# The build-time clock of VectorE's queue: new spacings and waits, and polynomial work filled up to a later limit

## The chip, the core and the metric

The kernel runs on one core of a Trainium2 chip. The metric is the device time of one execution in microseconds. Before the change it is 8143.15 us, the median of three runs between 8141.27 and 8144.12.

Five engines work beside each other, each in the order in which its instructions were written: TensorE (PE, with its weight loads as PEld), VectorE (DVE), ScalarE (ACT), GpSimd (POOL) and SyncE (SP), which issues most of the DMAs.

## What is computed

The input is x of 4 x 64 x 64 x 128 (batch, height, width, channels). Two layers follow each other; each image becomes 4096 tokens of 128 channels. Cut to what matters:

```python
# layer 0
c1 = conv3x3(elu(x), W1) + b1
a, b = split(conv3x3(c1, W2) + b2)
c3 = a * sigmoid(b)
q, k, v = c3 @ Wq + bq, c3 @ Wk + bk, c3 @ Wv + bv      # 4, 4 and 16 wide
x = x + c3 + tile(causal_softmax(q k^T / 4) @ v, 8) @ W3 + b3
# layer 1, on tokens
y = layernorm(x)
h = y + softmax(heads(y wq) heads(y wk)^T) heads(y wv) @ wo    # 16 heads of 8, not causal
t = x + h + (silu(h @ w1) * (h @ w3)) @ w2
z = layernorm(t)
p = softmax(z @ router_w + router_b)
out = t + sum over the two best experts e of p_e / (p_1 + p_2) * (z @ expert_w[e] + expert_b[e])
```

The costliest part is the exponential of the 16-head attention: 4 images x 16 heads x 4096 x 4096 scores.

## The kernel before

**The stream of attention steps.** The second attention is cut into segments. A segment is one image b, one group g of four heads and one chunk c of 512 queries. It has 32 steps, one for each tile of 128 keys; a few segments of the first image are shorter. A step multiplies four heads' keys with the queries (four matmuls into two PSUM tiles `s` of 128 x 1024), lets ScalarE take the exponential of both (`e<-s`), and, one or two steps later, multiplies values with `e` into the sum `acc`, which lies in one PSUM bank of its own. `s` has three buffers. The first attention's steps (36 for each image) go through the same stream.

**Polynomial.** In each segment of 32 steps, one key tile (number 20) is left out of ScalarE's work. Its exponential is worked out by VectorE instead: this is the class `Beside`. A job has four units, one for each head, and two halves. A unit is one matmul into the single bank `m` and one VectorE operation `ey<-m`; behind it eight steps on 128 x 512 elements are put on the list `beside_todo` (round off, fraction, to power, first, three terms, last). When all four units are ready, the two halves multiply the values with the four tiles `ey` into `acc`.

**Fillers.** All other work of the layers is written as Python generators, which yield between pieces: convolutions and first attention of the next image (`PREPARE`, 138.5 us of PE in the planner's units), and for each image and chunk a `last_part` (`LAST`, 18.3): output projection, gated feed-forward, LayerNorm, router, gates, experts. Within the stream, every piece of a filler uses the same single bank `m`. A yield names its cost and a kind: `held` (the bank is in use over the yield), `stop`, `free` (nothing on PE).

**The planner's turn.** The loop at the end of `fast_path` writes the order by hand while the program is built. A turn is one step; `turn_at` goes on by `EXPS`, 1.81 us. In a turn come, in this order: the scores of the step; one piece, either of a job (`can[0].piece()`) or of a filler (`insert()`); the values of an earlier step (`finish(2)`); the jobs' ages (`step()`); and `beside_work(until)`, which takes polynomial steps from the list as long as VectorE's clock plus the step's cost stays under `until`. A piece needs an empty bank (`empty`), some credit, and room on PE (`left >= PIECE`, or a credit over 1.5); in the first two turns of a segment none is issued (`quiet`). A half needs its polynomial to be done by the clock: `done_at <= turn_at[0] + 0.4`. Halves that are not out by the last step are forced there by `beside_rest`, and pieces that are left when the stream ends run alone.

**The clocks.** `InOrder` keeps each engine's instructions in the order written. For VectorE it calls `dve_time` at each instruction, which moves `dve_at`, the estimated end of VectorE's queue; `pool_time` does so for `pool_at`. `bank_at` is the estimated end of VectorE's last read of bank `m`. None of these puts a wait into the program; the semaphores for real dependencies are there in any case. They only settle which instruction comes where.

**Places that the text below uses.** `layernorm` (`ve`, then `rs` on GpSimd, then four operations that read `rs`); `top` and the gates in `last_part` (some 17 operations on 32 elements in front of the first `by_e`); the experts (`by_e<-m`, twice for each of four tiles, with a sum after the second); `elu` in the convolutions.

All trace lines carry L113, the line of the helper that records every instruction, so tiles name them.

Of the kernel before, what the change touches and what calls it, by code (L numbers as in the profile page):

```python
# [21 lines left out]
NQ = N // QB  # L22
# [103 lines left out]
def fast_path(ctx: ExitStack, tc: tile.TileContext, a: dict, where: dict, out: bass.AP, verdict):  # L126
# [7 lines left out]
    x = a["x"]  # L134
# [3 lines left out]
    turn_at, dve_at, pool_at, bank_at = [0.0], [0.0], [0.0], [0.0]  # L138

    def pool_time(name, args):  # L140

        aps = [x for x in args if hasattr(x, "shape")]
        if aps and name != "dma_start":
            took = 0.65 + 1.25e-3 * int(np.prod(aps[0].shape[1:]))
            pool_at[0] = max(pool_at[0], turn_at[0] + 0.5) + took

    def dve_time(name, args):

        aps = [x for x in args if hasattr(x, "shape")]
        from_bank = any(x.name.startswith("m_") or x.name == "m" for x in aps)  # L150
        from_sums = any(x.name.startswith("acc") for x in aps)
        in_sbuf = not any(x.space == bass.MemoryType.PSUM for x in aps)
        took = max(int(np.prod(x.shape[1:])) for x in aps[:2]) / 960.0
        if in_sbuf and name in ("tensor_scalar", "tensor_copy"):
            took *= 0.5
        if name == "tensor_reduce" and aps[1].ap[-1][0] != 1:
            took *= 1.8
        begins = turn_at[0] + (0.95 if from_bank else 1.75 if from_sums else 0.0)
        if in_sbuf and max(dve_at[0], begins) < pool_at[0]:
            took += 0.75  # L160
        dve_at[0] = max(dve_at[0], begins) + 0.07 + took
        if from_bank:
            bank_at[0] = dve_at[0]

    dve, pool = InOrder(tc, nc.vector, dve_time), InOrder(tc, nc.gpsimd, pool_time)

    const = ctx.enter_context(tc.tile_pool(name="f_const", bufs=1))
# [12 lines left out]
    def m_tile():  # L180
        return ps_m.tile([P, QB], FP, tag="m", name="m")
# [7 lines left out]
    def chunk(tag, name=None):  # L189
        return wk.tile([P, QB], FP, tag=tag, bufs=CHUNKS.get(tag, 1), name=name or tag)  # L190

    def small(name, dims):
        return sm.tile([P, *dims], FP, tag=name, name=name)

    def by_k(ap):
        return ap.rearrange("p (k c) -> p k c", k=4)
# [63 lines left out]
    acc = ps_o.tile([P, QB], FP, tag="acc", name="acc")  # L260
# [7 lines left out]
    bank_held = [False]  # L268

    def do_step(step):  # L270
        scores, values = step
        undone.append((values, scores()))

    def finish(leave):
        while len(undone) > leave:
            values, es = undone.pop(0)
            values(es)
# [10 lines left out]
    def insert():  # L288

        while fillers:  # L290
            r = advance(fillers[0])
            if r is not None:
                return r[0]
            fillers.pop(0)
        return 0.0

    def layernorm(t, y):

        t, y = by_k(t), by_k(y)
        mv = sm.tile([P, 4, 2], FP, tag="mv", name="mv")  # L300
        for k in range(4):
            st = sm.tile([P, 6], FP, tag="st", name="st")
            dve.bn_stats(st, t[:, k, :])
            dve.bn_aggr(mv[:, k, :], st)
        ve = small("ve", [4])
        dve.tensor_scalar(ve, mv[:, :, 1], LN_EPS, None, ALU.add)
        rs = small("rs", [4])
        pool.tensor_tensor(rs, ve, minus_half, ALU.pow)
        dve_at[0] += 1.2
        for k in range(4):  # L310
            dve.tensor_scalar(y[:, k, :], t[:, k, :], mv[:, k, 0:1], rs[:, k : k + 1], ALU.subtract, ALU.mult)

# [624 lines left out]
    beside_todo = []  # L937

    class Beside:
# [27 lines left out]
        def unit(self, j):  # L967
            ps = m_tile()
            r = slice(j * SLOT, (j + 1) * SLOT)
            pe.matmul(  # L970
                ps,
                lhsT=kx[r, self.place * P : (self.place + 1) * P].bitcast(FR),
                rhs=self.qx[r, :].bitcast(FR),
                start=True,
                stop=True,
            )
            y = chunk("ey")
            self.e.append(y)
            dve.tensor_scalar(y, ps, LOG2E, None, ALU.mult)
            low, a = [], [-((-1) ** k) * POWER[k] / float(np.float32(POWER[5])) for k in range(5)]  # L980

            def round_off():
                low.extend([chunk("em"), chunk("part", "eg")])
                dve.tensor_scalar(low[0], y, TO_WHOLE + EXPONENT, None, ALU.add)

            def fraction():
                dve.scalar_tensor_tensor(low[1], low[0], TO_WHOLE + EXPONENT, y, ALU.subtract, ALU.subtract)

            def to_power():
                whole = low[0].bitcast(mybir.dt.int32)  # L990
                dve.tensor_scalar(whole, whole, 23, MANTISSA, ALU.logical_shift_left, ALU.bitwise_or)

            def first():
                dve.scalar_tensor_tensor(y, low[1], a[4], low[1], ALU.add, ALU.mult)

            def term(k):
                return lambda: dve.scalar_tensor_tensor(y, y, a[k], low[1], ALU.add, ALU.mult)

            def last():
                dve.scalar_tensor_tensor(y, y, a[0], low[0], ALU.add, ALU.mult)  # L1000
                self.ready += 1
                self.done_at = dve_at[0]

            beside_todo.extend([(0.35, round_off), (0.6, fraction), (0.35, to_power), (0.6, first)])
            beside_todo.extend([(0.6, term(3)), (0.6, term(2)), (0.6, term(1)), (0.6, last)])

        def half(self, h):
            kt = self.kt
# [9 lines left out]
    def beside_work(until, beside_pool=True):  # L1018
        while beside_todo and dve_at[0] + beside_todo[0][0] <= until:
            if not beside_pool and max(dve_at[0], turn_at[0] + 0.5) < pool_at[0]:  # L1020
                break
            beside_todo.pop(0)[1]()
# [206 lines left out]
    batches = []  # L1229
# [121 lines left out]
    jobs = []  # L1351
# [107 lines left out]
    while True:  # L1459
        turn_at[0] += EXPS  # L1460
        if steps_in:
            do_step(steps_in.pop(0))
        else:
            step = next(steps, False)
            if step is False:
                break
            waiting = step is None
            if waiting:
                finish(0)
            else:  # L1470
                do_step(step)
        b = now[0]
        if batches[b].second == NQ and len(batches) == b + 1 and b + 1 < B:
            Batch(b + 1)
            begun = 0
            while begun < len(fillers) and (fillers[begun][2] in fetching or fillers[begun][2] is None):
                begun += 1
            fillers.insert(begun, [first_attention(b + 1, batches[b + 1]), PREPARE, None, False])

        rate = 1.0  # L1480
        if batches[b].second == NQ:
            later = PREPARE * (B - len(batches)) + LAST * (last_parts_left[0] - 1)
            rate = (sum(part[1] for part in fillers) + later) / max(1, sum(steps_left) - 40)
        credit = min(3.0, credit + rate)
        left = ahead + EXPS - SCORES - (VALUES if len(undone) > 2 else 0.0)
        free = bool(fillers) and fillers[0][3]
        turn = not quiet[0] and free and not waiting
        if turn:
            took = insert()
            credit -= took  # L1490
            left -= took
        can = [job for job in jobs if job.can() and (left >= PIECE or job.late())]
        empty = bank_held[0] or bank_at[0] <= turn_at[0] + 0.5 or batches[b].second < NQ
        if can and empty and not (quiet[0] or bank_held[0] or steps_in or waiting):
            can[0].piece()
            left -= PIECE
        elif not turn and (waiting or not quiet[0] and empty and credit > 0.0 and (left >= PIECE or credit > 1.5)):
            took = insert()
            credit -= took
            left -= took  # L1500
        ahead = min(max(left, 0.0), AHEAD)
        finish(2)
        for job in jobs:
            job.step()
        beside_work(turn_at[0] + 2.5, any(job.age > 3 * job.units + 4 for job in jobs if job.halves < 2))
    finish(0)
    alone[0] = True
    run_alone([(r for part in fillers for r in part[0])], lambda: False)
# [678 lines left out]
def conv_attn_hybrid_kernel(tc: tile.TileContext, a: dict, where: dict, out: bass.AP):  # L2187
    nc = tc.nc
    with tc.tile_pool(name="verdict", bufs=1) as pool:
        verdict = pool.tile([1, 1], FP, name="verdict")  # L2190
        fast_path(tc, a, where, out, verdict)

        beyond = nc.values_load(verdict.bitcast(mybir.dt.int32))
        with tc.If(beyond > 0x3F800000):
            general_path(tc, a, where, out)
# [30 lines left out]
```

## Time and profile before

| what | us |
|---|---|
| median of three runs | 8143.15 |
| the profiled execution | 8143.47 |
| its span, first to last instruction | 8141.6 |
| PE busy (73,465 matmuls) | 7864.7 |
| ACT busy (8,459 instructions) | 7690.0 |
| of it the exps `e<-s`, 8,256 | 7626.4 |
| DVE busy (9,289 instructions) | 4802.6 |
| POOL busy | 671.3 |
| granted TensorE clock | 0.988 |

The table gives busy time over the whole span. The stream of attention steps begins near 200 us and ends at 8049 us; ahead of it lie weights, the first bands of the convolution and the first chunks, behind it what is left of the fillers. PE's busy time overstates it, since matmuls are pipelined and their ends are modelled.

In the views, a wait line reads: engine and tile that waited, what released it, microseconds in total, how many times, the longest. A timeline line has start, duration, engine, operation, output and input, and in brackets the idle time before it with what ended it. `PEld` is a weight load, the first thing of a product that can wait.

### The profile page before, as it was taken

Reading aid. Unit: us, or ns where it says so; the run is one execution under the profiler, and the core shown is the slowest. Engines: PE = TensorE matmul, PEld = TensorE weight load, DVE = VectorE, ACT = ScalarE, POOL = GpSimd, SP = SyncE. Lnnn points to the kernel's source line nnn. Section 1 sums busy time; section 2 is a strip of 40 time slices with the busy share of each in tenths; the row PEclk is TensorE's granted clock in tenths of the full one; section 3 lists DMA queues with packets and bytes.
Section 4 is the critical chain, followed back from the end, with each engine's and each line's share of the span. In section 5 each row is a group of like instructions: output and inputs, shape, how many; then the busy total and the mean of one; then the engine's idle time right before and its main releaser. Section 6 shows DMA issues by size and latency. Waiting matters only on the chain. (4 is left out here: it accounts for less than half of the span.)

```text
span 8141.6 us, 177397 instructions
## 1 busy us (share of the span) xinstructions
PE 7864.7 (97%) x73465; PEld 2456.6 (30%) x73465; DVE 4802.6 (59%) x9289; ACT 7690.0 (94%) x8459; POOL 671.3 (8%) x592
## 2 busy tenths in 40 slices
PE   7999999999999999999999999999999999999997
PEld 3232222222232223223323222223233333333333
DVE  4333555463567666556656676655656666665666
ACT  1899999999999999999999999999999999999995
POOL 1211210100012110000002210000000000000000
PEclk9999999999999999999999999999999999999998
DMA  2221010101100101011010011101101111111221
GB/s 72 68 67 65 26 58 29 60 29 62 38 29 12 51 29 47 27 48 33 27 36 25 27 37 39 48 27 49 29 22 55 52 47 47 56 51 44 71 79 33
DMA packets 332340, 356.55 MB, mean 44 GB/s; under 512 B 146083, under 2 KB 222339, under 8 KB 331523
## 3 DMA queue, kind: packets, MB, share of 16 engines
q1 hardware_dynamic: 327507, 343.35, 13.3%
q8 instruction: 578, 9.47, 0.5%
q10 hardware_dynamic: 4016, 1.77, 0.1%
q14 instruction: 239, 1.96, 0.1%
HBM read 209.24 MB, written 135.79 MB: 42 GB/s over the span
## 5 line engine op out<-in xcount | busy, mean ns | idle before, releaser
L113 ACT ACTIVATE e<-s 128x1024 f32<-128x1024 f32 x8256 | 7626.4, 1085 | 222.7 <-PE s L113 214.9
L113 PE MATMUL acc<-e,vg 128*9 128x512 f32 x31872 | 4242.6, 597 | 3.4 <-DVE at L113 3.4
L113 PE MATMUL s<-qx,f_kx 32*128 32x512 f32 (+1 forms) x16512 | 2667.5, 496 | 38.5 <-DMA f_kx<-d_k 19.3
L113 PEld LDWEIGHTS s<-qx,f_kx 32*128 32x128 f32 (+1 forms) x16512 | 1080.2, 182 | 3883.5 <-ACT e L113 3612.8
L113 DVE SCALAR_TENSOR_TENSOR ey<-ey,eg 128x512 f32<-128x512 f32 x1344 | 953.9, 710 | 36.7
L113 PEld LDWEIGHTS acc<-e,vg 128*9 128x9 f32 x31872 | 727.8, 90 | 801.3 <-issue 407.2
L113 DVE COPY at<-acc 128x512 f32<-128x512 f32 x131 | 90.6, 691 | 662.4 <-PE acc L113 650.7
L113 PE MATMUL m<-v,f_wino 128*32 128x256 f32 x5376 | 429.8, 391 | 16.9 <-POOL v L113 7.3
L113 PE MATMUL m<-f_we,y2T 128*32 128x256 f32 x3840 | 308.9, 394 | 42.4 <-DVE by_e L113 28.2
L113 DVE TENSOR_SCALAR ey<-m 128x512 f32<-128x512 f32 x448 | 306.1, 683 | 68.9 <-PE m L113 65.5
L113 POOL TENSOR_TENSOR rs<-ve,f_minus_half 128x4 f32<-128x4 f32 x64 | 65.2, 1019 | 3168.5 <-DVE ve L113 3168.5
L113 DVE SCALAR_TENSOR_TENSOR ey<-ey,em 128x512 f32<-128x512 f32 x448 | 316.9, 707 | 10.2
L113 DVE SCALAR_TENSOR_TENSOR eg<-em,ey 128x512 f32<-128x512 f32 x448 | 313.2, 699 | 12.3
L113 DVE SCALAR_TENSOR_TENSOR ey<-eg 128x512 f32<-128x512 f32 x448 | 314.6, 702 | 0.0
L113 POOL TENSOR_TENSOR v<-r 128x1024 f32<-128x1024 f32 x112 | 220.6, 1975 | 1110.6 <-PE m L113 1110.1
L113 DVE COPY sd<-m 128x512 f32<-128x512 f32 x168 | 115.9, 690 | 278.3 <-PE m L113 277.4
L113 DVE TENSOR_TENSOR by_e<-m,gates 128x512 f32<-128x512 f32 x240 | 164.7, 686 | 163.8 <-PE m L113 160.1
L113 PE MATMUL m<-hT,f_fw 128*32 128x256 f32 (+1 forms) x2640 | 228.4, 391 | 0.1
L113 PE MATMUL m<-qx,f_kx 32*128 32x512 f32 x448 | 194.6, 434 | 25.1 <-DVE ey L113 23.7
L113 POOL TENSOR_TENSOR t<-t,h 128x512 f32<-128x512 f32 x32 | 43.5, 1360 | 2112.2 <-DVE h L113 2112.2
L113 DVE TENSOR_SCALAR em<-ey 128x512 f32<-128x512 f32 x448 | 196.6, 439 | 12.4
L113 DVE TENSOR_SCALAR em<-em 128x512 int32<-128x512 int32 x448 | 195.9, 437 | 10.2
(260 smaller groups left out, 4265.6 us busy)
## 6 DMA issues: line engine op xcount, KB each, us to landing
f_kx<-d_k SPq DMA_DIRECT2D x139, 512.0 KB
qx<-d_q SPq DMA_DIRECT2D x152, 256.0 KB
d_q<-two SPq DMA_DIRECT2D x64, 512.0 KB
d_a<-at SPq DMA_DIRECT2D x128, 256.0 KB
vg<-d_v SPq DMA_DIRECT2D x32, 576.0 KB
d_k<-two SPq DMA_DIRECT2D x32, 512.0 KB
d_v<-vc SPq DMA_DIRECT2D x32, 288.0 KB
xe<-in_x_dram SPq DMA_DIRECT2D x32, 256.0 KB
```

The lines of the kernel that those rows point to most:

```text
L113: made = op(*args, **kw)
```

## The change

`dve_time` gets other numbers and other cases:

- each operation costs 0.075 us beside its elements (0.07 before), and 0.117 more if it reads what the operation just before it on VectorE wrote;
- the factor of 1.8 for strided reductions is gone;
- an operation that reads bank `m` begins at 1.1 us of the turn (0.95 before), one that reads `acc` at 1.85 (1.75). New: one that reads `e` at 2.2, and LayerNorm's operations that read `rs` at 1.3 us after the estimated end of `ve` (before, `layernorm` added a flat 1.2 us to the clock);
- only inputs, no longer the output, decide of these cases;
- the supplement of 0.75 us beside GpSimd is given if the operation begins 0.2 us or more before GpSimd's end.

Six of the eight polynomial steps of each unit have a cost of 0.73 instead of 0.6 for the test in `beside_work`. The bank counts as empty if it is read by 0.3 us into the turn (0.5 before), and polynomial is filled up to 2.9 us instead of 2.5. The instructions themselves, their number and their operands stay as they are.

```diff
+    power_at, before = [0.0], [None]
+
     def dve_time(name, args):
 
         aps = [x for x in args if hasattr(x, "shape")]
-        from_bank = any(x.name.startswith("m_") or x.name == "m" for x in aps)
-        from_sums = any(x.name.startswith("acc") for x in aps)
+
+        def reads(prefix):
+            return any(x.name.startswith(prefix) for x in aps[1:])
+
+        from_bank = reads("m_") or any(x.name == "m" for x in aps[1:])
         in_sbuf = not any(x.space == bass.MemoryType.PSUM for x in aps)
         took = max(int(np.prod(x.shape[1:])) for x in aps[:2]) / 960.0
         if in_sbuf and name in ("tensor_scalar", "tensor_copy"):
             took *= 0.5
-        if name == "tensor_reduce" and aps[1].ap[-1][0] != 1:
-            took *= 1.8
-        begins = turn_at[0] + (0.95 if from_bank else 1.75 if from_sums else 0.0)
-        if in_sbuf and max(dve_at[0], begins) < pool_at[0]:
+        took += 0.075
+        if any(x.name == before[0] for x in aps[1:]):
+            took += 0.117
+        before[0] = aps[0].name
+        begins = 0.0
+        if from_bank:
+            begins = turn_at[0] + 1.1
+        elif reads("acc"):
+            begins = turn_at[0] + 1.85
+        elif reads("e_"):
+            begins = turn_at[0] + 2.2
+        elif reads("rs_") and name == "tensor_scalar":
+            begins = power_at[0] + 1.3
+        begins = max(dve_at[0], begins)
+        if in_sbuf and begins < pool_at[0] - 0.2:
             took += 0.75
-        dve_at[0] = max(dve_at[0], begins) + 0.07 + took
+        dve_at[0] = begins + took
+        if aps[0].name.startswith("ve_"):
+            power_at[0] = dve_at[0]
         if from_bank:
             bank_at[0] = dve_at[0]
...
         pool.tensor_tensor(rs, ve, minus_half, ALU.pow)
-        dve_at[0] += 1.2
...
-            beside_todo.extend([(0.35, round_off), (0.6, fraction), (0.35, to_power), (0.6, first)])
-            beside_todo.extend([(0.6, term(3)), (0.6, term(2)), (0.6, term(1)), (0.6, last)])
+            beside_todo.extend([(0.35, round_off), (0.73, fraction), (0.35, to_power), (0.73, first)])
+            beside_todo.extend([(0.73, term(3)), (0.73, term(2)), (0.73, term(1)), (0.73, last)])
...
-        empty = bank_held[0] or bank_at[0] <= turn_at[0] + 0.5 or batches[b].second < NQ
+        empty = bank_held[0] or bank_at[0] <= turn_at[0] + 0.3 or batches[b].second < NQ
...
-        beside_work(turn_at[0] + 2.5, any(job.age > 3 * job.units + 4 for job in jobs if job.halves < 2))
+        beside_work(turn_at[0] + 2.9, any(job.age > 3 * job.units + 4 for job in jobs if job.halves < 2))
```

## The prediction

> **What bounds the kernel now.** I read the page's busy table first, then busy time by stretch of the span, then the waits, then single stalls in the timeline. The table alone says little (PE 97%, ACT 94%). By stretch it is clear:
>
> ```profile
> core 0: us, PE busy (x) PEld busy (x) DVE busy (x) ACT busy (x) POOL busy (x), PEclk, DMA share, GB/s
> 2000.00:3000.00 1000.00, 968.66 (x8992) 292.69 (x8992) 660.42 (x1192) 967.24 (x1062) 135.16 (x103) 0.99 0.10 31
> 6000.00:7000.00 1000.00, 984.79 (x9920) 309.55 (x9916) 625.18 (x1242) 986.30 (x1088) 21.09 (x25) 1.00 0.16 48
> 8050.00:8141.60 91.60, 51.81 (x210) 39.07 (x208) 56.78 (x151) 4.24 (x8) 3.56 (x5) 0.73 0.08 24
> ```
>
> ACT is 97 to 99% busy while the stream of attention steps runs, 4% in the last 91.6 us. The number of exps is fixed, and the change alters none of it. So the time can move in two places: ACT's holes in the stream, and the tail after it. The waits from 400 to 8050 us name the holes:
>
> ```profile
> PEld s L113 <- ACT e L113: 3525.4, 4867, 1.7
> ACT e L113 <- PE s L113: 162.6, 126, 9.3
> ...
> PE m L113 <- DVE ey L113: 51.0, 69, 4.6
> PE acc L113 <- DVE ey L113: 38.7, 22, 4.6
> PE m L113 <- DVE by_e L113: 28.2, 23, 2.3
> ```
>
> The first line is health: PE waits for ACT at most steps. The second is the whole room inside the stream. The last three are its cause: PE, in order, stands behind a product that needs the one bank m (still unread by VectorE) or a finished polynomial tile ey. By stage the same view gives ACT 94.6 us from 1500 to 5500 and 41.0 from 5500 to 8050, which leaves 162.6 - 94.6 - 41.0 = 27.0 before 1500; 9.6 of that is a DMA (f_kx). One such stall, at the expert gates:
>
> ```profile
> 4180.73 0.19 DVE L113 TENSOR_TENSOR aw<-aw,pr 128x32 f32<-128x32 f32 x1
> 4180.84 0.15 DVE L113 TENSOR_TENSOR am<-am,bm 128x4 f32<-128x4 f32 x1
> 4181.03 0.18 DVE L113 RECIPROCAL am<-am 128x4 f32<-128x4 f32 x1
> 4181.24 0.19 DVE L113 TENSOR_TENSOR gates<-aw,am 128x32 f32<-128x32 f32 x1
> 4181.54 0.31 DVE L113 STREAM_TRANSPOSE turned<-gates 128x128 f32<-128x128 f32 x1
> 4181.77 0.65 DVE L113 TENSOR_TENSOR by_e<-m,gates 128x512 f32<-128x512 f32 x1
> ...
> 4182.48 0.16 PEld L113 LDWEIGHTS m<-f_we,y2T 128*32 128x32 f32 x8 [2.58 <-DVE by_e L113]
> ...
> 4185.46 1.94 ACT L113 ACTIVATE e<-s 128x1024 f32<-128x1024 f32 x2 [3.11 <-PE s L113]
> ```
>
> PE was sent to the bank while VectorE still worked through 17 small operations in front of by_e (4178.05 to 4181.77, 3.72 us). PE stood 2.58 us, ACT 3.11.
>
> **What the Trainium skill says.** "Perfetto Trace Analysis", section Identifying the Most-Contended Engine, warns that matmul busy time is a poor measure of the limit; the 3525.4 us above agree. "VectorE: DVE Perf Modes", section The DRAIN you can't avoid, has each operation wait until the pipe of the one before is empty; here small operations of 0.19 us start 0.22 to 0.23 us apart, and the three polynomial terms from 2756.47 take 2.14 us. "Advanced Engine Details and Errata", section VectorE Performance Modes, says that GpSimd and two-port Vector operations block each other; here tensor_scalars of 128x128 that run beside GpSimd's row terms take about 1.2 us (4.84 for four at 2747.29), against 342 ns for y on average.
>
> **The change, part by part.** No operation is added or removed; only the order of VectorE's polynomial steps and the turns in which bank pieces are issued move. No wait is added either. A piece that moves a turn takes its DMAs on SP's queue (y, gates, sums, out) and its GpSimd terms with it; in the stream these have turns to spare, so they cost only the turn.
>
> *Durations.* A 512-wide scalar_tensor_tensor costs the planner 0.533 + 0.07 = 0.603 us before, 0.533 + 0.075 + 0.117 = 0.725 after if it reads the previous result. A unit's eight polynomial steps: 4.29 before (two of 0.337, six of 0.603), 4.92 after; the trace has 5.12 (2754.22 to 2759.34). The gate chain: 1.8 before (14 of 0.103 and three others), about 3.9 after (13 dependent ones of 0.033 + 0.075 + 0.117 = 0.225, and four others of 0.7 together), 3.72 in the trace. So the old clock runs 16% fast in the polynomial and by half in the chain; the new one is right within 5%.
>
> *Filling to 2.9.* The next bank read is assumed at 1.81 + 1.1 = 2.91 us, so polynomial ends just before it. In the old clock a full turn gets 1.81 us of estimated work, really 2.1 us, in a turn of 1.90 real ones (62 turns in 118.0 us); VectorE then lags. With the new one it doesn't. The longer limit and the dearer steps about cancel: I cost this edit by itself at 0, bounds -20 to +20 us, since VectorE is 62% busy.
>
> *Gain.* ACT's 162.6 us less the DMA's 9.6 leaves 153. The polynomial waits (38.7 of the 117.9 us of PE stalls listed) come from done_at being early; that clock is mended. Gate and unit stalls come from bank_at being early; also mended. What stays: LayerNorm beside GpSimd, where the clock has 1.3 + 3.57 us and the trace 1.14 + 4.84, and forced polynomial at a segment's end. I take 70%: 107 us, bounds 50% (77) and 85% (130).
>
> *Loss.* A stall avoided is a turn in which the piece is not issued, as the bank counts as full. Fillers have few turns to spare: from 7100 to 8045 each last part takes exactly two segments, 62 turns, and nearly every turn but the quiet ones and those waiting for DMA carries a bank piece. At 8044 a last part has only just begun; so it and the final one run alone in the tail:
>
> ```profile
> 8044.18 0.69 DVE L113 TENSOR_TENSOR h<-m,h 128x512 f32<-128x512 f32 x1 [6.84 <-PE m L113]
> ...
> 8089.53 0.39 SPq L113 DMA_DIRECT2D out_dram<-t  x1
> ...
> 8134.45 0.40 SPq L113 DMA_DIRECT2D out_dram<-t  x1
> ```
>
> Alone, a last part takes 8134.45 - 8089.53 = 45 us, so each turn lost while fillers are saturated costs 45/62 = 0.73 us at the end. Now count by hand. Gate chain: VectorE's clock stands near 1.1 when it starts, 5.0 after it, 5.6 after by_e; the bank is called empty at 1.81k + 0.3, so at k = 3; before it was about 3.4 against 1.81k + 0.5, k = 2. One turn lost. A unit right after an expert's sums: 1.1 + 0.608 + 0.725 + 0.459 + 0.325 + 0.325 = 3.54, in the next turn 1.73, the unit ends at 2.34, over 2.11, so one turn lost; before 1.69 under 2.31. That makes 2 turns for each last part. From 5500 on 21.5 last parts run: 43 turns, 31 us. Earlier, 9 last parts (18 turns) and two preparations of a batch, where I guess 12 turns each from the elu chunks beside GpSimd: 42 turns, 31 us. There some turns go unused with the bank free, so I let a third be absorbed: 21. Bounds for the loss: 15 (all early ones absorbed, one turn each) to 155 (below).
>
> *The rest.* Expecting e_ at 2.2 only orders the first attention's masks, rs at power_at + 1.3 replaces a flat 1.2, and the 1.8 for strided reductions goes: together under 5 us either way.
>
> Sum: 8143.5 (profiled execution; span 8141.6 and 1.9 around it, 0.3 above the median of 8143.15) - 107 + 31 + 21 = 8089, so 8090.
>
> **Rivals.**
>
> *A, stalls go, some turns are lost* (0.55): 8090, own range 8050 to 8125. For it: the new spacings match the trace, and 118 us of PE stalls stand behind exactly the two estimates mended. Against: the tail.
>
> *B, the filler turns bind and the tail grows* (0.32, slower): with a stricter bank test and a slower clock, units and LayerNorms hold the bank too, so 5 turns are lost per last part (30.5, 152) and 30 per preparation (60). 212 turns by 0.73 is 155 us against 107: +48, 8191. It decides from 107/0.73 = 147 lost turns, 4% of the 3,450 since 1500. For it: the locked period of 62 turns, and a last part that had barely begun at the end. Against: a lost turn often replaces a stall that was longer than a turn anyway.
>
> *C, both cancel* (0.09): stages after 5500 gain 0.7 x 41 = 29 and lose 31; if the earlier ones do likewise, 8143.
>
> *D, polynomial becomes late* (0.04): fewer steps per turn push halves to the segment's end. Now they run mostly 8 to 20 us before it, two jobs in 112 at 2 us; if 20 more are forced at 2 us each, 40 us come back, 8130, which is no measurable change. Names that do not match the prefixes would leave the clock half mended; the old prefixes had the same form, so I give it no share of its own.
>
> **How the numbers follow.** Faster by over 0.2% (16 us, about what this kernel's measurement can tell from none) is A: 0.55. Within 0.2% are C and D: 0.13. Slower is B: 0.32. The range leaves out the best tenth of A and the worse half of B: 8045 to 8180.
>
> **What would show it.** Right: ACT's waits on PE s from 400 to 8050 near 55 us, PE's acc and by_e waits under 10 us each, the stream ending about 8049 - 107 = 7942, the tail near 145 us instead of 92. Gate turns followed by two without a bank piece instead of one. Wrong: a stream that ends after 8020 (the clock was not what made the stalls), or a tail over 200 us (B); a tail still at 92 would make it better than forecast, some 8035.

## The result, and the profile after

The changed kernel takes 8028.25 us (median of four runs, 8024.68 to 8032.38) against 8143.52 on the same chip. The ratio is 0.9859 with a 95% interval of 0.9842 to 0.9876: 115 us or 1.4% faster. The forecast of 8090 had the sign; the time lies below its range, which began at 8045.

First the same stretches of the changed kernel. Columns as before; the last stretch begins 0.4 us after the last exp ends.

```profile
core 0: us, PE busy (x) PEld busy (x) DVE busy (x) ACT busy (x) POOL busy (x), PEclk, DMA share, GB/s
2000.00:3000.00 1000.00, 991.87 (x9213) 300.79 (x9213) 676.49 (x1219) 994.97 (x1094) 134.53 (x103) 1.00 0.11 32
6000.00:7000.00 1000.00, 998.12 (x10077) 315.17 (x10077) 637.92 (x1282) 998.59 (x1107) 20.61 (x26) 1.00 0.17 51
7903.30:8022.80 119.50, 67.63 (x281) 50.39 (x275) 77.60 (x203) 4.47 (x9) 4.84 (x6) 0.74 0.11 31
```

ACT now stands 0.1 to 0.5% of these stretches, where it stood 1.4 to 3.3%. The exps are as many; 1094 instead of 1062 ACT instructions lie in the first stretch. The last line is the other account: the tail has grown. With the end of the last exp as the border, the stream ended at 8047.4 us and left a tail of 94.2; now it ends at 7902.9 and leaves 119.9. So the stream gave 144.5 us, the tail took 25.7, and 118.8 is the difference of the spans.

The waits of the changed kernel from 400 us to the stream's end (who waits for whom: microseconds, times, longest):

```profile
PEld s L113 <- ACT e L113: 3563.9, 4970, 1.7
...
ACT e L113 <- PE s L113: 38.3, 28, 9.4
...
PE acc L113 <- DVE ey L113: 6.9, 5, 2.1
PE m L113 <- DVE f_e_band L113: 5.8, 3, 2.4
PE m L113 <- DVE yT L113: 5.3, 4, 2.8
PE m L113 <- DVE at L113: 3.9, 21, 0.2
```

ACT's waits fall from 162.6 us (126 times) to 38.3 (28 times). PE's waits for the gates' by_e (28.2) are gone from the list; those for a polynomial tile fall from 38.7 to 6.9, those for a bank read by ey from 51.0 to 3.1. The longest wait left, 9.4 us, is the DMA of f_kx.

The gates again, of a later last part, in the timeline of the changed kernel (start, duration, engine, operation, output and input; in brackets the idle time before):

```profile
7107.17 7.70 ACT L113 ACTIVATE e<-s 128x1024 f32<-128x1024 f32 x8
...
7108.05 0.64 PE L113 MATMUL m<-f_we,y2T 128*32 128x256 f32 x8
...
7109.70 0.31 DVE L113 STREAM_TRANSPOSE turned<-gates 128x128 f32<-128x128 f32 x1
...
7109.91 1.05 PE L113 MATMUL acc<-e,vg 128*9 128x512 f32 x8
7109.93 0.65 DVE L113 TENSOR_TENSOR by_e<-m,gates 128x512 f32<-128x512 f32 x1
...
7110.89 0.87 PE L113 MATMUL s<-qx,f_kx 32*128 32x512 f32 x4
...
7111.69 0.16 PEld L113 LDWEIGHTS m<-f_we,y2T 128*32 128x32 f32 x8 [0.25 <-issue]
```

The same chain of small operations still makes by_e late. But the next product into bank m (7111.69) now lies a turn later, behind another step's scores, and finds the bank empty. Eight exps run through without a hole. The turn between them, at 7109.48, carries no piece: this is the lost turn that the forecast counted for the gates. Within the stream, 26 of 29 last parts show one such empty turn in the changed kernel; in the kernel before, 29 of 30 show none, and PE goes to the bank in the very next turn.

### The profile page after: what moved, and what is told of

Its sections match the earlier page's. It is cut to its first block, busy times and chain, and to the rows that moved or that the text cites. A ratio compares the mean times of both kernels' runs of the same rounds, so it can differ in the third digit from the quotient of the medians.

```text
span 8022.8 us, 177192 instructions
## 1 busy us (share of the span) xinstructions
PE 7846.5 (98%) x73321; PEld 2465.8 (31%) x73321; DVE 4813.6 (60%) x9289; ACT 7673.7 (96%) x8459; POOL 675.6 (8%) x592
## 5 line engine op out<-in xcount | busy, mean ns | idle before, releaser
L113 ACT ACTIVATE e<-s 128x1024 f32<-128x1024 f32 (+1 forms) x8256 | 7610.1, 1095 | 96.8 <-PE s L113 90.3
L113 DVE TENSOR_TENSOR t<-m,t 128x512 f32<-128x512 f32 x59 | 40.8, 692 | 331.0 <-PE m L113 331.0
```

What stands on the lines that cost most here:

```text
L113: made = op(*args, **kw)
```

## The experiments

The stream's end and the tail are taken from each profile as above. ACT's waits are those on `s` from 400 us to the stream's end. The time is the median of the runs, the ratio is against the kernel before the change on the same chip. That kernel took 8145.34 us on the chip of runs 1 to 4, 8144.86 on that of runs 5 to 8 and 8144.16 on that of run 9, so a few microseconds between two rows mean little.

| run | time, us | ratio (95% interval) | stream's end | tail | ACT's waits |
|---|---|---|---|---|---|
| before | 8143.52 | | 8047.4 | 94.2 | 162.6 |
| changed | 8028.25 | 0.9859 (0.9842 to 0.9876) | 7902.9 | 119.9 | 38.3 |
| 1, new clock alone | 8050.54 | 0.9882 (0.9866 to 0.9899) | 7930.7 | 121.4 | 61.2 |
| 2, new limits alone | 8236.78 | 1.0112 (1.0095 to 1.0129) | 8135.8 | 105.8 | 250.1 |
| 3, no 0.117 | 8140.14 | 0.9994 (0.9985 to 1.0003) | 8048.0 | 93.4 | 161.7 |
| 4, changed, pieces at any credit | 7975.27 | 0.9792 (0.9776 to 0.9808) | 7904.2 | 67.2 | 33.3 |
| 5, changed, 66 late turns held back | 8093.98 | 0.9937 (0.9920 to 0.9954) | 7902.4 | 189.2 | 39.6 |
| 6, changed, 66 early turns held back | 8035.59 | 0.9865 (0.9849 to 0.9882) | 7912.4 | 122.2 | 42.7 |
| 7, changed, old begins | 8051.49 | 0.9886 (0.9870 to 0.9903) | 7928.7 | 120.7 | 59.0 |
| 8, changed, bank test at 0.5 | 8042.00 | 0.9874 (0.9857 to 0.9890) | 7916.9 | 122.5 | 41.5 |
| 9, before, pieces at any credit | 8108.76 | 0.9956 (0.9939 to 0.9973) | 8039.6 | 66.9 | 150.5 |

The planner's turns can be counted while it writes the program. Of 4,126, it leaves without a piece, and for no other reason than that bank m counts as full: 6 before, 85 in the changed kernel, 59 in run 1, 18 in run 2 and 19 in run 3. The runs that hold few turns back are those that keep the stalls.

### 1. The new clock without the new limits

```diff
-beside_work(turn_at[0] + 2.9, ...
+beside_work(turn_at[0] + 2.5, ...
-bank_at[0] <= turn_at[0] + 0.3
+bank_at[0] <= turn_at[0] + 0.5
-(0.73, fraction) and the five others
+(0.6, fraction) and the five others
```

> The new clock with the old limits: steps tested at 0.6, bank empty by 0.5, polynomial up to 2.5. Theory 1 (the clock's truth removes the stalls, and the limit of 2.9 only keeps the polynomial from coming late): in the order written, 50 halves are now forced at a segment's end against 3 in the changed kernel, so some 25 segments end on unfinished polynomial at 2 to 5 us each; bank stalls stay gone. PE's by_e waits under 10 us, its acc<-ey waits 60 to 120 us; time 8080 to 8150. Theory 2 (the fuller filling brought the gain, the clock nothing): as before the change, 8143, with by_e waits still near 28 us. Theory 3 (the bank test at 0.3 brought it): 8143 as well, with by_e waits near 28 us.

Measured 8050.54 us, faster than any theory had it. Waits for by_e are gone, as theory 1 said, and PE's waits for a polynomial tile in acc are 12.1 us, not 60 or more. So forced halves mostly find their polynomial done: 50 were forced, in 28 segments, and nine waits were seen. The clock alone brings 95 of the 115 us. Theories 2 and 3 fall.

### 2. The new limits without the new clock

```diff
-beside_work(turn_at[0] + 2.5, ...
+beside_work(turn_at[0] + 2.9, ...
-bank_at[0] <= turn_at[0] + 0.5
+bank_at[0] <= turn_at[0] + 0.3
-(0.6, fraction) and the five others
+(0.73, fraction) and the five others
```

> The old clock with the new limits: 0.73, 0.3 and 2.9. Theory 1: the clock still runs 16% fast in the polynomial and by half in the gate chain, and 2.9 packs VectorE fuller, so it lags more; by_e waits stay over 20 us, PE's ey waits stay at 90 us or grow; time 8130 to 8180. Theory 2 (filling): 8030. Theory 3 (the bank test): by_e and unit waits fall to less than half, time 8050 to 8090.

Measured 8236.78 us, 91 slower than before and worse than the worst expectation. The waits from 400 us to the stream's end, PE's and ACT's of this kernel:

```profile
PE m L113 <- DVE ey L113: 71.9, 68, 2.8
PE m L113 <- DVE by_e L113: 45.4, 45, 2.9
PE acc L113 <- DVE ey L113: 41.1, 19, 5.3
...
ACT e L113 <- PE s L113: 250.1, 194, 9.4
```

All three of PE's waits on VectorE grow against before, although the bank test is stricter. This fits theory 1: a clock that runs fast, given a later limit, puts more polynomial in front of the next bank read than VectorE can do in time. That it is the later limit among the three is not shown.

### 3. The change without the term for dependent operations

```diff
-            took += 0.117
+            took += 0.0
```

> The changed kernel without the 0.117 us for an operation that reads the one before it; waits, limits and bank test stay. Theory 1: this one term is most of the clock's mending (16% in the polynomial, half of the gate chain), so half or more of the gain goes: by_e waits back over 15 us, time 8080 to 8140. Rival (the waits 1.1, 1.85, rs carry it): 8025 to 8050.

Measured 8140.14 us: the interval of the ratio holds 1. ACT's waits are 161.7 us, those of before. So without this one number nothing of the gain is left, more than theory 1 had said ("half or more"); the time is 0.1 us beyond what it expected.

```profile
PE m L113 <- DVE ey L113: 42.5, 61, 2.9
PE m L113 <- DVE by_e L113: 32.9, 38, 2.2
PE acc L113 <- DVE ey L113: 19.8, 16, 3.9
```

The three waits are back: 95 us together, against 118 before and 10 in the changed kernel. That does not make the term the whole of the clock: run 2 lacks it too and takes 97 us more than this run, so beside the new limits the other parts of the new clock count as well. The shares of the parts do not add up, and the term alone, in the kernel before, was not tried.

### 4. The change, with filler pieces at any credit

```diff
-... and (left >= PIECE or credit > 1.5)):
+... and credit > 0.0):
```

> The changed kernel, with a filler's piece allowed at any positive credit (before: 1.5, or room on PE by the planner). 64 more filler pieces are issued within the stream, by the planner's own order. Theory 1 (the tail is unfinished filler work at 0.73 us a turn): the tail falls by 64 x 0.73 = 47 us from 119 to about 73, the stream grows by under 8 us; time 7975 to 7995. Rival (pieces without room on PE hold up the exps as much as they save later, or the last parts wait for their segments): 8020 to 8040.

Measured 7975.27 us, 53 less than the changed kernel and the best of all. The stream's end moves by 1.3 us; the tail goes from 119.9 to 67.2. ACT in the last stretch of this run:

```profile
7894.59 9.59 ACT L113 ACTIVATE e<-s 128x1024 f32<-128x1024 f32 x10
7925.71 0.63 ACT L113 ACTIVATE th<-h 128x512 f32<-128x512 f32 x1 [21.53 <-DVE h L113]
7928.53 0.63 ACT L113 ACTIVATE th<-h 128x512 f32<-128x512 f32 x1 [2.18 <-DVE h L113]
7931.30 0.63 ACT L113 ACTIVATE th<-h 88x512 f32<-88x512 f32 x1 [2.14 <-DVE h L113]
7946.10 0.23 ACT L113 ACTIVATE pr<-lg 128x32 f32<-128x32 f32 x1 [14.17 <-DVE lg L113]
```

One set of tanh and one router's exp: a single last part is left, that of the last segment, which can't begin earlier. In the changed kernel the tail holds two sets of tanh and the end of a third last part. The rival falls.

### 5 and 6. What a lost turn costs

```diff
+        turns[0] += 1
+        empty = empty and not (LOW <= turns[0] < LOW + 990 and turns[0] % 15 == 0)
```

LOW is 3000 in the first of these runs, 600 in the second.

> The changed kernel, with pieces held back in 66 more turns: every 15th from turn 3000 to 3989, where the fillers have no turns to spare. By the planner's own order 62 filler pieces fewer lie in the stream. Theory 1 (a turn lost there comes back in the tail at 0.73 us): tail +45 us, stream unchanged within 8 us, time 8065 to 8080. Rival (a lost turn costs nothing, as the stream gets shorter by what the piece took on PE): 8020 to 8035. Rival (a lost turn costs a whole turn of 1.87 us): 8145.

Measured 8093.98 us, 66 more than the changed kernel and 14 beyond the expectation. The stream's end is the same within 0.5 us; the tail grows by 69.3. The 28th last part began (its first h) at step 4,070 of the stream, against 3,977 in the changed kernel: a lag of 93 steps, and 69.3 / 93 is 0.745 us. So the price holds for a step of lag. The expectation took each missing piece for one step, and that was wrong: in the changed kernel each late last part takes exactly 62 steps, two segments, but they hold only some 41 filler pieces (738 in the 1,126 turns from turn 3,000 on). At this rate the 62 missing pieces are 95 steps; with turns held back most last parts take 66 to 75. A missing piece cost 69.3 / 62 = 1.12 us.

> The same 66 turns held back, from turn 600 to 1589, where the planner still leaves turns empty for want of room or credit. By the planner's own order the number of filler pieces in the stream is that of the changed kernel. Theory 1: nothing is lost, 8020 to 8036. Rival (every lost turn costs 0.73 us wherever it lies): 8076.

Measured 8035.59 us, inside the expectation. The tail grows by 2.3 us. The 28th last part begins at step 3,977, as in the changed kernel: early turns are made up. The stream ends some 9 us later; the reason is not shown.

### 7. The old begins

```diff
-            begins = turn_at[0] + 1.1
+            begins = turn_at[0] + 0.95
-            begins = turn_at[0] + 1.85
+            begins = turn_at[0] + 1.75
-            begins = turn_at[0] + 2.2
+            begins = 0.0
-            begins = power_at[0] + 1.3
+            begins = power_at[0] + 1.2
```

> The changed kernel with the old begins: bank 0.95, sums 1.75, e from 0, LayerNorm 1.2 after ve; durations, limits and bank test stay new. Theory 1 (the durations of dependent operations carry the gain, the begins little): 8010 to 8050. Rival (the begins carry a third or more of it): 8065 to 8100.

Measured 8051.49 us, 1.5 over theory 1's upper end: beside the rest of the change, the begins are worth 23 of the 115 us. PE's waits for a polynomial tile are 18.3 us (11 times), against 6.9.

### 8. The old bank test

```diff
-bank_at[0] <= turn_at[0] + 0.3
+bank_at[0] <= turn_at[0] + 0.5
```

> The changed kernel with the bank called empty by 0.5 us again. Theory 1: 27 fewer turns are held back by the planner, each for a short stall of up to 0.2 us that the step's slack partly hides; stream +0 to +10 us, filler pieces unchanged by the planner's order; time 8025 to 8045. Rival (the test at 0.3 is a main part of the gain): 8060 to 8100.

Measured 8042.00 us, as expected: 14 us, and the stream ends 14.0 later, although ACT's waits grow by only 3.2. Some of it lies ahead of the view and is not the edit's: in this profile the first exp starts at 75.1 us against 72.0, in a part of the program that is the same in both, and by 400 us 207 exps have begun against 213, some 5.5 us. Where the rest comes from is not shown.

### 9. Pieces at any credit, in the kernel before

```diff
-... and (left >= PIECE or credit > 1.5)):
+... and credit > 0.0):
```

> The kernel before the change with a filler's piece allowed at any positive credit, as in the run of the changed kernel with that edit. By the planner's order 69 more filler pieces lie in the stream, and 17 halves are forced at a segment's end against 4. Theory 1 (tail and stalls are separate accounts): the tail falls from 94 to about 67, what the final last part needs alone, the stalls stay (ACT's waits on PE s 160 to 190 us up to the stream's end); time 8110 to 8135. Rival (this edit brings by itself most of what it brought together with the clock): under 8090.

Measured 8108.76 us, 35 less than before, 1 below the expectation. The tail falls by 27.3 us to 66.9, the same floor as in run 4 (what the final last part takes alone); the stream gets 7.8 shorter, with ACT's waits at 150.5, under the 160 expected. So the two accounts are separate: this edit takes the tail to its floor, the change takes the stalls. With the tail at its floor in both, runs 9 and 4, the stream ends 135.4 us earlier with the change. Since both tails stop at the floor, 64 pieces are worth 52.7 us there and 69 are worth 27.3 here; these two runs give no price for a piece, and run 4's 47 us came near by luck.

## Why the prediction was right, and where it was wrong

**The two accounts: right.** It said that time can move in ACT's holes and in the tail, that the holes shrink and the tail grows. Both happened, and runs 4, 5 and 9 move the tail with the stream's end held within 8 us. The sizes of both were off, and with them the range.

**The clock: right, and more so.** "The new one is right within 5%" in the polynomial and the gate chain: with the 0.117 us taken out, the gain is gone (run 3). For the chain the prediction's own terms sum to 3.6 us and not to "about 3.9"; the planner's clock gives 3.64, against 3.72 in the trace. The trace of the kernel before shows the term itself, in VectorE's operations of one unit:

```profile
2754.22 0.43 DVE L113 TENSOR_SCALAR em<-ey 128x512 f32<-128x512 f32 x1
2754.68 0.69 DVE L113 SCALAR_TENSOR_TENSOR eg<-em,ey 128x512 f32<-128x512 f32 x1
2755.41 0.43 DVE L113 TENSOR_SCALAR em<-em 128x512 int32<-128x512 int32 x1
2755.75 0.68 DVE L113 SCALAR_TENSOR_TENSOR ey<-eg 128x512 f32<-128x512 f32 x1
```

The second line needs em and starts 0.46 us after the first em operation; the second em operation, the third line, takes the same 0.43 us, and the last line, which doesn't need it, starts after 0.34. It holds throughout: the medians are 0.461 us in 358 pairs of the first kind and 0.342 in 374 of the second.

**Filling to 2.9: near the edge of its bounds.** Costed at 0 with -20 to +20. It was not tried by itself. With the new clock, all three limits together are worth some -20 us (a gain of 115 us against 95 in run 1); with the old clock +91 (run 2). What the limits do depends on whether the clock is true.

**Gain: the mechanism was right, the size too small.** "I take 70%: 107 us, bounds 50% (77) and 85% (130)." Measured 144.5, above the upper bound. Two parts of this sum were off. The share was 81%: ACT's waits fell by 124.3 of the 153 us, inside the bounds. And the 153 itself was short. In the kernel before:

```profile
2744.13 11.16 ACT L113 ACTIVATE e<-s 128x1024 f32<-128x1024 f32 x12
```

The twelve exps take 11.16 us, 0.92 apart, while each is shown with 1.09. The profiled windows of two exps in a row overlap by about 0.18 us. "Perfetto Trace Analysis", section DVE / Act Engine Instruction, has the window end with the acknowledged write, while the next instruction may begin to fetch its data before that; the overlap in this trace agrees. So the idle time in front of an exp, as the view counts it, is 0.18 us shorter than what the hole cost. 98 waits fewer by 0.18 is 18 us, and 124.3 + 18 is 142 of the 144.5. ACT's busy time from 400 us to the stream's end shows these 18 us, kernel before first:

```profile
400.00:8047.45 7647.45, 7479.81 (x70984) 2290.88 (x70982) 4590.07 (x8801) 7477.26 (x8217) 587.10 (x488) 0.99 0.14 43
400.00:7902.90 7502.90, 7447.46 (x70772) 2290.37 (x70768) 4581.02 (x8750) 7459.40 (x8215) 590.11 (x487) 1.00 0.14 43
```

With two instructions fewer of 8,217, ACT is busy 17.9 us less, since each hole that closes lets two windows overlap again. What is left of these stretches is idle time; it fell by 126.7 us, and the two together are the stream's gain.

**Loss: the count was near, what a held-back turn costs was not.** The forecast counted 43 + 42 = 85 held-back turns, 24 of them a guess; the planner holds back 79 more than before. It priced a lost turn at 0.73 us, as one step of lag: the tail grew by 25.7 for 35 steps (the 28th last part begins at step 3,977 instead of 3,942), 0.73 each, and run 5 gives 0.745. What failed is to take each held-back turn for one step of lag: "2 turns for each last part. From 5500 on 21.5 last parts run: 43 turns, 31 us", as if all of these reached the end, and "I let a third be absorbed" for the earlier ones. From turn 3,000 on, 32 turns are held back, about two for each last part, as counted; but 80 pieces of the polynomial jobs now lie in turns in which the filler has nothing for PE, against 58 before, and the number of filler pieces is 738 against 735. Nothing was lost there. The late last part keeps its 62 steps. Between turns 1,000 and 3,000, 41 more are held back and 22 filler pieces fewer are issued; here the lag arose. At the rate of run 5, 22 pieces are 34 steps. So most held-back turns cost nothing, and one that costs a piece costs more than was forecast, 25.7 / 22 = 1.17 us. That the early part is where turns are to spare was the wrong way round, except for turns 600 to 1,589, which run 6 shows to be free.

**The sum.** 8089 - (144.5 - 107) - (52 - 25.7) = 8025, and the profiled execution of the changed kernel takes 8024.68. These two terms are the whole error.

**The rivals.** B, the tail outweighs the stalls, needed 147 lost turns; a lag of 35 steps came. Its mechanism is real: run 5 has 93 more steps of lag and gives back more than half of the gain. C falls. D, late polynomial, is what run 1 was expected to show; 50 forced halves cost little there (12.1 us of PE's waits in acc, against 6.9). Of its signs, "ACT's waits near 55 us" was 38.3, "the stream ending about 7942" was 7902.9, "the tail near 145" was 119.9. PE's acc waits (6.9) and by_e waits (none listed) came under 10 as described. The gates got the one turn more that was counted, but it is one empty turn where there was none, not two where there was one.

**Open.** Which of the three limits does the harm with the old clock was not tried; nor was what fixes the late last part at exactly two segments.

## What to carry to other kernels

Where a build-time plan orders one engine's work in front of another's waits, the plan's clock has to be right in the small terms: here 0.117 us per dependent operation decided on 1.4% of the time, and the new limits on top of a fast clock cost 1.1%. Split such a change into two accounts, the holes of the engine that bounds the stream and the work left behind its end, and price a lost piece of work by what it costs in the second; a held-back turn costs nothing if other work can take its place. And when idle time in front of a pipelined engine's instructions is added up, check the distance between two undisturbed starts against the shown duration: the difference belongs to each hole.

## What the runs showed of the hardware that was not expected

In these traces an exp of 128 x 1024 is shown with 1.09 us and follows the one before at 0.90 to 0.92 us when nothing disturbs it. A VectorE operation of 0.43 us lets an independent successor start after 0.34 us and a dependent one after 0.46.
